# A four-layer conv/attention kernel: layer 0's products with v stored by channel instead of by row

## The chip, the cores and the metric

The kernel runs on one core of a Trainium2 chip. A core has five engines that work side by side, each with its own list of instructions: PE (TensorE, matmuls), DVE (VectorE, elementwise work and sums along a row), ACT (ScalarE, activations and copies), POOL (GpSimd, which here issues the indirect gathers) and SP (SyncE, which here issues plain DMAs). They wait for each other only through semaphores. On-chip memory (SBUF) has 128 partitions; an instruction of DVE works on all 128 at once and walks through the elements of each partition one after the other. PSUM is the small memory that PE writes into.

The metric is the device time of one execution in microseconds (us). Its median over 15 runs is 9,851.63 us before the change (9,807.8 to 9,883.81). A profile is taken in one more execution.

## What is computed

An input of 4 images, 64 x 64 pixels, 128 channels, float32, runs through four layers. The change is in layer 0, a deformable attention with 4 groups of 32 channels. For each pixel and group, 9 sampling points are displaced by learned offsets; each is interpolated from its 4 neighbouring pixels. The reference for it, cut to what matters:

```python
k_list, v_list = ([], [])
for i in range(G):                                  # G = 4 groups
    off = conv1x1(pconv(q_img, pconv_off_w[i]), w_off[i], b_off[i])
    dil = 2 * i + 1
    k_list.append(deform_sample(kv[0, :, i], off, mask, dil, dil * PAD))
    v_list.append(deform_sample(kv[1, :, i], off, mask, dil, dil * PAD))
...
attn = jax.nn.softmax(jnp.einsum('bgnc,bgckn->bgnk', qf, ks_), axis=-1)
out = jnp.einsum('bgnk,bgckn->bgnc', attn, vs_)
```

`deform_sample` gathers four corners for each of the K2 = 9 points and adds them up with bilinear weights. The kernel never forms the samples: for the scores it multiplies q with all 9 x 4 = 36 gathered rows of k, weighs the 36 sums and adds each four; for the output it multiplies the 36 gathered rows of v with 36 weights (softmax numerator times corner weight) and adds them up. Layers 1 to 3 (linear attentions, a mixture of experts, a spectral filter) follow, image by image.

## The kernel before

**Staging.** `hybrid` runs the images b = 0 to 3 one after the other through layer 0. For each there are 8 chunks (c) of 8 image rows, each with 4 tiles (t) of 128 pixels, each with 4 groups (g): 128 groups an image, 512 in all. `attend` handles one tile and yields after each group. At each yield `hybrid` inserts pieces of other work: the layers 1 to 3 of the image before (`Post.run(b - 1)`), or weight preparation while b is 0. After image 3's layer 0, layers 1 to 3 of image 3 run alone. `front(b + 1)` (group norm and convolutions of the next image, which fill the table that is gathered from) is inserted too.

**One group in `attend`.** POOL issues 9 indirect DMAs (L609), one for each sampling point; each fetches for 128 pixels 256 floats: 4 corners of 32 k values and 32 v values. They land in `gt`, a tile from a pool of three buffers, so the gathers run up to three groups ahead and then wait until DVE has read a buffer for the last time. DVE then does, in this order:

- `pr` (L618): k half of `gt` times q, 36 x 32 products
- `s4` (L623): sum over the 32 channels, 36 results, a reduction over elements that lie side by side
- L624, L626, L628: corner weights, sum over corners, and the maximum `mx`
- ACT makes `ex` = exp(sc - max) (L632)
- `aw` (L636): `ex` times corner weights, 36 weights, written into the PSUM tile `qa`
- `pv` (L641): v half of `gt` times `aw`, 36 x 32 products. This is the last reader of `gt`
- `o` (L644): sum over the 36 rows for each of 32 channels

A tile's last group is followed by the division by `den` (L649, L651). `pr` and `pv` live in a pool with one buffer each (`self.t1`). The tile framework sets the order in each engine's list; as built, DVE's list has the `pr` of the next group between `pv` and `o`, and the next group's `s4` right behind `o`. All arithmetic is float32.

**Order on ACT.** While the spectral filter of layer 3 runs beside layer 0, the class `Turns` keeps an order on ACT between the filter's copies (`y`, L1419, from PSUM to SBUF) and `ex`: each `ex` is issued after the last ACT instruction of the other work inserted before it, and each `y` after the last `ex`.

**Layout of the products.** `pv` is a tile of 36 rows of 32 channels: a row i of 32 floats, then the next. The product is written in that order, side by side. The sum walks it by channel: for each channel the 36 rows, 32 floats (128 bytes) apart.

**Other lines spoken of.** In `where`, the corner weights `cw` (L571) are written at every 4th float and `my` (L561) at every 2nd; `ix` (L549) reads two inputs at every 2nd float. L962 and L212 are memsets by DVE: of one float in each 129 (32 of them), and of two full rows of 66. L246 reads one input at every 9th float. L1405 and L1429 are PE's two kinds of matmul in the spectral filter.

Of the kernel before, what the change touches and what calls it, by code (L numbers as in the profile page):

```python
# [8 lines left out]
F32 = mybir.dt.float32  # L9
I32 = mybir.dt.int32  # L10
AF = mybir.ActivationFunctionType
ALU = mybir.AluOpType
AX = mybir.AxisListType
# [3 lines left out]
P = 128  # L17
# [13 lines left out]
K2 = 9  # L31
# [147 lines left out]
class Layer0:  # L179
# [416 lines left out]
    def attend(self, b, c, t):  # L596

        nc = self.nc
        blk = self.blk[b, c]
        o = blk.o  # L600

        qa = blk.qa[t // 2]
        q0 = t % 2 * C
        den = self.sm.tile([P, G], F32, tag="den", name="den")
        for g in range(G):
            gt = self.gp.tile([P, K2, 256], F32, tag="gt", name="gt")
            for i in range(K2):
                col = g * K2 + i
                nc.gpsimd.indirect_dma_start(  # L609
                    out=gt[:, i, :], out_offset=None, in_=self.tbl[b % 2][:, :],  # L610
                    in_offset=bass.IndirectOffsetOnAxis(
                        ap=blk.idx[:, t, col : col + 1], axis=0
                    ),
                )
            corners = gt.rearrange("p i (c s) -> p (i c) s", c=4)
            cw = blk.cw[:, t, g * K2 : (g + 1) * K2, :]
            pr = self.t1.tile([P, 4 * K2, 32], F32, tag="pr", name="pr")
            nc.vector.tensor_mul(  # L618
                pr, corners[:, :, 0:32],
                qa[:, q0 + 32 * g : q0 + 32 * g + 32].unsqueeze(1).to_broadcast([P, 4 * K2, 32]),  # L620
            )
            s4 = self.sm.tile([P, 4 * K2], F32, tag="s4", name="s4")
            nc.vector.tensor_reduce(s4, pr, AX.X, ALU.add)  # L623
            nc.vector.tensor_mul(s4, s4, cw.rearrange("p i c -> p (i c)"))  # L624
            sc = self.sm.tile([P, K2], F32, tag="sc", name="sc")
            nc.vector.tensor_reduce(sc, s4.rearrange("p (i c) -> p i c", c=4), AX.X, ALU.add)  # L626
            mx = self.sm.tile([P, 1], F32, tag="mx", name="mx")
            nc.vector.tensor_reduce(mx, sc, AX.X, ALU.max, negate=True)  # L628
            ex = self.sm.tile([P, K2], F32, tag="ex", name="ex")
            with self.turns.after("behind"):  # L630
                self.turns.mark()
                nc.scalar.activation(ex, sc, AF.Exp, bias=mx, accum_out=den[:, g : g + 1])  # L632
            self.turns.took("samples")
            a0 = 2 * C + g % 2 * 4 * K2
            aw = qa[:, a0 : a0 + 4 * K2]
            nc.vector.tensor_mul(  # L636
                aw.rearrange("p (i c) -> p i c", c=4), cw,
                ex.unsqueeze(2).to_broadcast([P, K2, 4]),
            )
            pv = self.t1.tile([P, 4 * K2, 32], F32, tag="pv", name="pv")  # L640
            nc.vector.tensor_mul(  # L641
                pv, corners[:, :, 32:64], aw.unsqueeze(2).to_broadcast([P, 4 * K2, 32]),
            )
            nc.vector.tensor_reduce(  # L644
                o[:, t, 32 * g : 32 * g + 32], pv.rearrange("p i s -> p s i"), AX.X, ALU.add
            )
            if g < G - 1:
                yield
        nc.vector.reciprocal(den, den)  # L649
        og = o[:, t, :].rearrange("p (g c) -> p g c", g=G)  # L650
        nc.vector.tensor_mul(og, og, den.unsqueeze(2).to_broadcast([P, G, 32]))  # L651
        yield
# [1186 lines left out]
```

## Time and profile before

| | us |
|---|---|
| median of 15 runs | 9,851.63 |
| lowest, highest | 9,807.8, 9,883.81 |
| the profiled execution | 9,820.63 |
| its span, first to last instruction | 9,818.9 |

The busy time of the engines in five stretches (the images of layer 0, and what lies around them), with the TensorE clock that the chip granted (1 is full speed):

| stretch, us | what runs | PE | DVE | ACT | POOL | PE clock |
|---|---|---|---|---|---|---|
| 0 to 278 | first front, tables | 216 | 49 | 100 | 29 | 0.98 |
| 278 to 1,935 | image 0 of layer 0, weights, front | 404 | 922 | 104 | 1,097 | 0.60 |
| 1,935 to 4,150 | image 1; layers 1 to 3 of image 0 | 1,463 | 1,090 | 578 | 1,103 | 0.79 |
| 4,150 to 6,358 | image 2; layers 1 to 3 of image 1 | 1,480 | 1,105 | 583 | 1,100 | 0.80 |
| 6,358 to 8,536 | image 3; layers 1 to 3 of image 2 | 1,292 | 1,089 | 550 | 1,076 | 0.74 |
| 8,536 to 9,819 | layers 1 to 3 of image 3 | 1,032 | 380 | 337 | 0 | 0.87 |

How to read what follows: a *group* of instructions is all that come from one line with one operation; its row gives the count, the busy time, the mean duration in ns, and the time that the engine stood idle right before them, with what ended it ("<-"). A row of the *waits* says who waited, for whom, how long in total, how many times, and the longest. "remote" means that the profile knows no instruction that released the wait. No engine is busy all the time; how long an instruction takes matters only where something waits for it.

### The profile page before, as it was taken

Reading aid. Unit: us, or ns where it says so; the run is one execution under the profiler, and the core shown is the slowest. Engines: PE = TensorE matmul, PEld = TensorE weight load, DVE = VectorE, ACT = ScalarE, POOL = GpSimd, SP = SyncE. Lnnn points to the kernel's source line nnn. Section 1 sums busy time; section 2 is a strip of 40 time slices with the busy share of each in tenths; the row PEclk is TensorE's granted clock in tenths of the full one; section 3 lists DMA queues with packets and bytes.
Section 4 is the critical chain, followed back from the end, with each engine's and each line's share of the span. In section 5 each row is a group of like instructions: output and inputs, shape, how many; then the busy total and the mean of one; then the engine's idle time right before and its main releaser. Section 6 shows DMA issues by size and latency. Waiting matters only on the chain.

```text
span 9818.9 us, 86706 instructions
## 1 busy us (share of the span) xinstructions
PE 5886.1 (60%) x30155; PEld 4073.1 (41%) x30155; DVE 4635.5 (47%) x7777; ACT 2252.1 (23%) x4160; POOL 4405.9 (45%) x4736
## 2 busy tenths in 40 slices
PE   7455100046675677746675767743455777657899
PEld 6242000035344555525344555522144555435676
DVE  1555555565464444466464444466354444343222
ACT  3100000023122222223122222213122222242222
POOL 0666666755534545555534554555435555300000
PEclk9677555567887888878787888865677888877999
DMA  6444333335645444445645444454635444434322
GB/s 214 141 126 118 104 102 101 102 99 149 204 129 144 117 117 119 112 134 157 190 139 146 114 122 114 114 134 133 193 110 149 118 111 115 133 106 126 107 69 80
DMA packets 1130830, 1255.00 MB, mean 128 GB/s; under 512 B 392478, under 2 KB 923161, under 8 KB 1126169
## 3 DMA queue, kind: packets, MB, share of 16 engines
q1 hardware_dynamic: 906797, 644.20, 24.0%
q0 software_dynamic: 221184, 604.27, 21.3%
q8 instruction: 239, 3.92, 0.2%
q14 instruction: 198, 1.62, 0.1%
q10 hardware_dynamic: 2412, 0.98, 0.0%
HBM read 1061.76 MB, written 187.22 MB: 127 GB/s over the span
## 4 chain that ended last, share of the span: by engine, by line
PE 23%; another core or an unknown queue 12%; ACT 5%; issue 5%; DVE 5%; DMA 3%; SPq 0%; POOL 0%; DVEq 0%; ACTq 0%
PE pa L1429 10%; PE pq L1405 4%; ACT y L1419 2%; DMA xin<-x 1%; PE ph L1114 1%; PE pm L427 1%; DVE o L644 1%; ACT ln L147 1%; PE pa L1225 0%; PE pn L1235 0%; PE pt L727 0%; PE pt L1123 0%; PE pq L862 0%; DVE pr L618 0%
## 5 line engine op out<-in xcount | busy, mean ns | idle before, releaser
L609 POOL DMA_INDIRECT gt<-tbl,idx x4608 | 4396.9, 954 | 4067.1 <-DVE pv L641 2280.2
L1429 PE MATMUL pa<-y,m 128*128 128x256 f32 x8192 | 2132.1, 411 | 239.2 <-issue 231.1
L1429 PEld LDWEIGHTS pa<-y,m 128*128 128x128 f32 x8192 | 1625.2, 204 | 725.0 <-issue 496.4
L1419 ACT COPY y<-pq 128x1024 f32<-128x1024 f32 x896 | 869.1, 1015 | 2365.0 <-remote 1401.0
L636 DVE TENSOR_TENSOR qa<-cw,ex 128x36 f32<-128x36 f32 x512 | 104.6, 204 | 2370.8 <-ACT ex L632 2223.6
L1405 PE MATMUL pq<-th,xh 32*128 32x256 f32 x8192 | 698.7, 442 | 642.1 <-ACT y L1419 402.3
L644 DVE TENSOR_REDUCE o<-pv 128x32 f32<-128x1152 f32 x512 | 1075.9, 2101 | 9.0 <-DVE qa L636 3.5
L618 DVE TENSOR_TENSOR pr<-gt,qa 128x1152 f32<-128x1152 f32 x512 | 690.5, 1349 | 224.2 <-DMA gt<-tbl,idx 208.1
L427 PE MATMUL pm<-wd,xT 128*128 128x256 f32 x2376 | 639.8, 420 | 252.7 <-ACT kv L438 142.4
L1405 PEld LDWEIGHTS pq<-th,xh 32*128 32x128 f32 x8192 | 422.5, 204 | 868.5 <-ACT y L1419 450.8
L641 DVE TENSOR_TENSOR pv<-gt,qa 128x1152 f32<-128x1152 f32 x512 | 691.9, 1351 | 40.1 <-DVE qa L636 12.8
L623 DVE TENSOR_REDUCE s<-pr 128x36 f32<-128x1152 f32 x512 | 688.3, 1344 | 1.8 <-DVE qm L874 0.9
L427 PEld LDWEIGHTS pm<-wd,xT 128*128 128x128 f32 x2376 | 487.4, 212 | 377.3 <-ACT kv L438 161.2
L632 ACT ACTIVATE ex<-sc,mx 128x9 f32<-128x9 f32 x512 | 156.9, 307 | 1170.3 <-DVE mx L628 519.4
L1416 DVE COPY y<-pq 128x1024 f32<-128x1024 f32 x128 | 156.7, 1225 | 466.1 <-ACT y L1419 466.1
L460 PE MATMUL pm<-xT,wd 128*128 128x512 f32 x576 | 296.1, 656 | 133.1 <-ACT qo L477 50.9
L578 PE MATMUL qa<-sident,qt 128*128 128x128 f32 x256 | 53.4, 334 | 423.8 <-issue 216.6
L1114 PE MATMUL ph<-w,pooled 128*1 128x512 f32 x512 | 244.0, 759 | 65.4 <-DMA w<-in_L_ffn_weight_dram 49.5
L502 PE MATMUL pm<-q,weff 128*81 128x512 f32 x192 | 137.7, 858 | 199.2 <-ACT xr L670 110.7
L660 PE MATMUL pt<-ident,o 128*128 128x128 f32 x128 | 36.1, 381 | 354.6 <-DVE o L651 144.3
L147 ACT ACTIVATE ln<-xin,ln,ln 128x128 f32<-128x128 f32 x512 | 211.6, 483 | 127.4 <-DMA xin<-x 99.4
L1128 DVE TENSOR_TENSOR g<-pt,b1T 128x16 f32<-128x16 f32 x64 | 11.2, 176 | 476.6 <-PE pt L1123 368.8
(373 smaller groups left out, 6322.0 us busy)
## 6 DMA issues: line engine op xcount, KB each, us to landing
w<-in_L_ffn_weight_dram SPq DMA_DIRECT2D x512, 256.0 KB
th<-th SPq DMA_DIRECT2D x512, 256.0 KB
gt<-tbl,idx POOLq DMA_INDIRECT x4608
xin<-x SPq DMA_DIRECT2D x256, 256.0 KB
x<-xin SPq DMA_DIRECT2D x160, 256.0 KB
tbl<-kv SPq DMA_DIRECT2D x264, 128.0 KB
th<-wx SPq DMA_DIRECT2D x32, 1024.0 KB
q<-qd SPq DMA_DIRECT2D x288, 64.0 KB
```

Of the source, the lines that this page charges most:

```text
L147: self.nc.scalar.activation(dst, src, AF.Identity, bias=self.shift[:, i : i + 1], scale=self.rstd[:, i : i + 1])
L427: nc.tensor.matmul(pm[:, t, :], lhsT=self.xf[:, at : at + P], rhs=self.wd[:, tap, C:], start=(t == 0 and tap == 0), stop=False,)
L460: nc.tensor.matmul(pv, lhsT=self.wd[:, tap, :C], rhs=self.xT[:, 8 * c + dy : 8 * c + dy + 8, dx : dx + HW], start=(tap == 0), stop=False,)
L609: nc.gpsimd.indirect_dma_start(out=gt[:, i, :], out_offset=None, in_=self.tbl[b % 2][:, :], in_offset=bass.IndirectOffsetOnAxis(ap=blk.idx ...
L618: nc.vector.tensor_mul(pr, corners[:, :, 0:32], qa[:, q0 + 32 * g : q0 + 32 * g + 32].unsqueeze(1).to_broadcast([P, 4 * K2, 32]),)
L623: nc.vector.tensor_reduce(s4, pr, AX.X, ALU.add)
L641: nc.vector.tensor_mul(pv, corners[:, :, 32:64], aw.unsqueeze(2).to_broadcast([P, 4 * K2, 32]),)
L644: nc.vector.tensor_reduce(o[:, t, 32 * g : 32 * g + 32], pv.rearrange("p i s -> p s i"), AX.X, ALU.add)
L1114: nc.tensor.matmul(ph[32 * j : 32 * j + 1, :], lhsT=pooled[:, 16 * j + q : 16 * j + q + 1], rhs=w1s[j], start=True, stop=True,)
L1405: nc.tensor.matmul(pq[:, r // 2, r % 2, :, pair, :], lhsT=xh[rows, 2 * (q % 4) + pair, :], rhs=t[rows, 2 * (q % 2) + pair, :].rearrange("p ...
L1419: nc.scalar.copy(to, src)
L1429: nc.tensor.matmul(pa[:, h * 2 * P : (h + 1) * 2 * P].rearrange("p (g x) -> p g x", g=8), lhsT=s.m[u][:, KC * kc + i, :], rhs=yv[:, i], st ...
```

## The change

`pv` becomes a tile of 32 rows (channels) of 36 elements. The product still goes through `gt` row by row, 36 rows of 32, but writes each element into its channel's row: one channel and the next lie 36 floats (144 bytes) apart. The sum then reads, for each channel, 36 elements that lie side by side. Inputs, sizes, results and the order of the additions stay the same.

```diff
-            pv = self.t1.tile([P, 4 * K2, 32], F32, tag="pv", name="pv")
+            pv = self.t1.tile([P, 32, 4 * K2], F32, tag="pv", name="pv")
             nc.vector.tensor_mul(
-                pv, corners[:, :, 32:64], aw.unsqueeze(2).to_broadcast([P, 4 * K2, 32]),
-            )
-            nc.vector.tensor_reduce(
-                o[:, t, 32 * g : 32 * g + 32], pv.rearrange("p i s -> p s i"), AX.X, ALU.add
-            )
+                pv.rearrange("p s i -> p i s"), corners[:, :, 32:64],
+                aw.unsqueeze(2).to_broadcast([P, 4 * K2, 32]),
+            )
+            nc.vector.tensor_reduce(o[:, t, 32 * g : 32 * g + 32], pv, AX.X, ALU.add)
```

## The prediction

> **What bounds the kernel now.** I read the costliest groups first, then the waits, then one stretch of the timeline, then the shapes that show what strides cost. Columns of a group: busy us, mean ns of one | idle us before it.
>
> ```profile
> L609 POOL DMA_INDIRECT gt<-tbl,idx x4608 | 4396.9, 954 | 4067.1 <-DVE pv L641 2280.2
> ...
> L644 DVE TENSOR_REDUCE o<-pv 128x32 f32<-128x1152 f32 x512 | 1075.9, 2101 | 9.0 <-DVE qa L636 3.5
> ...
> L641 DVE TENSOR_TENSOR pv<-gt,qa 128x1152 f32<-128x1152 f32 x512 | 691.9, 1351 | 40.1 <-DVE qa L636 12.8
> L623 DVE TENSOR_REDUCE s<-pr 128x36 f32<-128x1152 f32 x512 | 688.3, 1344 | 1.8 <-DVE qm L874 0.9
> ```
>
> The two sums read 1152 elements each. L623 reads them side by side: 1.344 us. L644 reads them 128 bytes apart (32 floats): 2.101 us. DVE is busy 47% of the span, so the 0.757 us between them is worth something only where DVE is what the others wait for. The waits (us in total, times, longest):
>
> ```profile
> POOL gt L609 <- DVE pv L641: 2280.2, 264, 111.4
> DVE qa L636 <- ACT ex L632: 2223.6, 268, 22.4
> ACT y L1419 <- remote: 1401.0, 153, 20.2
> ...
> ACT ex L632 <- DVE mx L628: 519.4, 66, 26.8
> ...
> ACT ex L632 <- DVE sc L626: 140.9, 21, 11.4
> ```
>
> It is a circle: the gathers on POOL wait for pv, which frees one of three gt buffers; pv's weights (qa) wait for ex on ACT; ACT's y stands ahead of ex in its queue and waits for something that has no name here. One turn of it in the timeline (start, us, what, idle before):
>
> ```profile
> 3312.65 1.35 DVE L641 TENSOR_TENSOR pv<-gt,qa 128x1152 f32<-128x1152 f32 x1
> ...
> 3314.28 0.95 POOL L609 DMA_INDIRECT gt<-tbl,idx  x1 [4.81 <-DVE pv L641]
> ...
> 3335.50 0.94 POOL L609 DMA_INDIRECT gt<-tbl,idx  x1 [0.30 <-issue]
> 3339.36 1.93 ACT L1419 COPY y<-pq 128x1024 f32<-128x1024 f32 x2 [19.70 <-remote]
> ...
> 3345.37 0.32 ACT L632 ACTIVATE ex<-sc,mx 128x9 f32<-128x9 f32 x1
> ...
> 3345.80 0.20 DVE L636 TENSOR_TENSOR qa<-cw,ex 128x36 f32<-128x36 f32 x1 [19.34 <-ACT ex L632]
> 3346.04 1.35 DVE L641 TENSOR_TENSOR pv<-gt,qa 128x1152 f32<-128x1152 f32 x1
> ...
> 3347.66 0.94 POOL L609 DMA_INDIRECT gt<-tbl,idx  x1 [11.22 <-DVE pv L641]
> ```
>
> pv ends at 3314.00, POOL starts 0.27 us later and issues 18 gathers, 1.25 us from start to start, to 3336.44. Only 2.9 us after its last one does y start, though the matmuls it reads had ended at 3320.1 by their rows. Then y, ex, qa, pv, and POOL starts again 33.4 us after the start before. In the stretch behind the last gather (8,536 us to the end) the list of ACT's waits has no "remote" entry at all; y waits there for PE by name. So I read: while gathers are under way a finished matmul often tells ACT so only when they have run dry. What the mechanism is, no row shows. But it puts pv on the path: a pv that ends d us later starts the gathers d later, and they end d later, and ex, and the next pv.
>
> The sum o (L644) isn't on that circle. DVE's order is pv, pr of the next group, o, s of the next group, three small ones, together 1.35+1.35+2.10+1.34+0.54 = 6.7 us, and the next group's nine gathers take 9 x 1.25 = 11.25 us. Where o's length does reach the path is where ex waits for DVE's mx or sc: 66 + 21 = 87 times.
>
> **The change part by part.** *Nothing moves.* Every engine's list of instructions is the same in number and order; only the 512 pv and 512 o change shape. No DMA, no wait is added or taken away, and pv takes as many bytes.
>
> *The sum o becomes a side-by-side read.* 1152 elements, as L623: 2.101 to 1.344 us, gain 0.757 each, 388 us of DVE work in 512. It reaches the path at the 87 waits above: 87 x 0.757 = 66 us. Bounds: 0 (hidden under the gathers everywhere) and 98 us (ex also waits 9 times for s of L623 and 34 times for nothing named, in the same list: 130 x 0.757). All 388 us can't be had while DVE idles half of the span.
>
> *The product pv writes across.* It reads as before, but each element now lands 144 bytes (36 floats) from the one before. The trace has no such write; the nearest rows:
>
> ```profile
> L571 DVE TENSOR_TENSOR cw<-up,my 128x144 f32<-128x144 f32 x64 | 23.3, 421 | 0.0
> ...
> L561 DVE TENSOR_TENSOR my<-up,mk 128x144 f32<-128x144 f32 x32 | 9.6, 302 | 0.0
> L549 DVE SCALAR_TENSOR_TENSOR ix<-fl 128x144 f32<-128x144 f32 x32 | 9.6, 301 | 0.0
> ...
> L962 DVE MEMSET ln<- 128x32 f32 x4 | 0.3, 85 | 0.0
> ...
> L212 DVE MEMSET xT<- 128x132 f32 x1 | 0.2, 168 | 0.0
> ```
>
> All have 144 elements but the memsets. L571 writes every 4th float (16 bytes apart): 421 to 426 ns. L561 writes every 2nd: 302. L549 reads two inputs at every 2nd and writes side by side: 301. So reads at every 2nd float are free, writes too, and the write at every 4th costs (423 - 302) / 144 = 0.84 ns an element. For 1152 elements that is 0.97 us: pv would take 2.32 us. From the other side, L962 writes 32 floats 516 bytes apart in 85 ns, just what a memset of 32 in a row would take (60 ns for two, 168 for 132: 0.83 ns each): there the wide write is free, and pv would stay at 1.35. Between them lies the price of the wide read, 0.657 ns an element or 0.757 us. I take 0.97, since L571 is the same operation on the same engine, with two inputs; a memset reads nothing. Upper end: twice that, 1.94 us, in case 144 bytes cost more than 16; nothing shows it, but L644's 128-byte read costs no more an element than the 36-byte read of L246 (371 ns for 128 against 286 for a side-by-side one: 0.66 ns), so distance beyond the first step hardly counts for reads.
>
> The Trainium skill has a rule that speaks against this change, in "Advanced Engine Details and Errata", section "Memory Cachelines": SBUF works in 16-byte lines, and an access that doesn't hit a line at least twice in a row pays. It makes no difference between reads and writes, so by it the write across pays as the read across did; it gives no figure. Priced like the read, the sum below would be 208 x 0.757 - 66 = +91 us rather than +136.
>
> *Where pv's price lands.* POOL waits for pv 264 times, 24 of them in batch 0 (up to 1,935 us, where POOL mostly issues without a break and is itself the bound at 11.25 us a group) and 240 in batches 1 to 3. Not all 264 turns are closed by a late "remote"; the 153 waits of y are those surely so, and in the others PE's own work may hide a later gather. I take the middle, 208 (bounds 153 and 264): 208 x 0.97 = +202 us. Behind pv in DVE's queue everything up to o comes 0.97 later, and behind o only 0.97 - 0.757 = 0.21 later; the 4.5 us by which 11.25 exceeds 6.7 cover that. Were that cover gone, it would be 0.21 us in each of 512 groups, 109 us.
>
> *The sum:* +202 - 66 = +136 us. The profiled execution took 9,820.6 us (span 9,818.9), so 9,957; it lies 31 us under the median of the 15 runs, 9,851.6. Against the median: **9,988, say 9,990 us**. Ends, if the write costs at least what the read did: 153 x 0.757 - 98 = +18 and 264 x 0.97 = +256, so 9,870 to 10,108.
>
> **The rivals.**
> *A, writes across are free* (as L962's). Then o's gain alone remains, on the 87 waits: 9,852 - 66 = 9,786, faster. The memset speaks for it, 128 cw instructions against. It decides the sign wherever the price of pv is under 66 / 208 = 0.32 us, a third of cw's price. Chance 0.20.
> *B, it comes out even:* the write costs about what the read did and PE, at a granted clock of 0.74 to 0.80 in batches 1 to 3, is what really closes most turns, so neither edit reaches the path: 9,852. For it: PE is busy 1,463 of 2,215 us in batch 1. Against: y waits for no named matmul 153 times. Chance 0.13.
> *C, the far write is dearer than the 16-byte one:* pv +1.94, 208 x 1.94 - 66 = +338, 10,190, and DVE's own chain reaches 7.9 us a group, still under 11.25. Against it: reads show no such growth. Chance 0.07.
> *That the change doesn't do what it says:* L623 shows the very read that o becomes, so I give it no share of its own.
>
> **How the numbers follow.** The forecast (slower, by pv's place on the circle) has 0.60, C 0.07, B 0.13, A 0.20. About 0.2% (20 us) is what a measurement of this kernel can tell from no change: faster 0.20, same 0.13, slower 0.67. Predicted time: the forecast's, 9,990. Range: from 9,800, which leaves out the larger half of A, to 10,090, which leaves out C and the last 18 us of the forecast's own range; the forecast's own range is 9,870 to 10,108.
>
> **What would show it.** pv (L641) at 2.1 to 2.4 us and o (L644) at 1.34; DVE's busy time up by about 109 us to 4,745; some 260 waits of POOL for pv, and its idle time up by over 100 us; a group of batches 1 to 3 from 17.2 us ((8,536 - 1,935) / 384) to about 17.5; the last 1,283 us, behind the last gather, as before. It is wrong if pv stays under 1.7 us (then A), or if pv is over 2.1 us and the time doesn't move (then the circle isn't closed by the gathers and B holds).

## The result and the profile after

| | before | after |
|---|---|---|
| median, us | 9,848.58 (31 runs) | 9,982.17 (6 runs) |
| lowest, highest | 9,807.8, 9,883.81 | 9,969.76, 9,995.17 |
| span of the profiled execution | 9,818.9 | 9,982.0 |

The ratio is 1.0137, with a 95% interval of 1.012 to 1.0154: the change makes the kernel 133.6 us slower. The forecast was 9,990 us, from 9,800 to 10,090.

The costliest groups of the kernel after, from its page (busy us, mean ns of one | idle us before it):

```profile
L609 POOL DMA_INDIRECT gt<-tbl,idx x4608 | 4406.5, 956 | 4221.5 <-DVE pv L641 2277.0
...
L641 DVE TENSOR_TENSOR pv<-gt,qa 128x1152 f32<-128x1152 f32 x512 | 1130.1, 2207 | 27.5 <-issue 9.6
...
L623 DVE TENSOR_REDUCE s<-pr 128x36 f32<-128x1152 f32 x512 | 688.4, 1344 | 4.1 <-issue 2.3
L645 DVE TENSOR_REDUCE o<-pv 128x32 f32<-128x1152 f32 x512 | 686.0, 1340 | 3.3 <-DVE qa L636 1.2
```

The sum o now costs what the other side-by-side sum (L623) costs, 0.761 us less than before; pv costs 0.856 us more. On DVE the two nearly cancel: 512 x 0.095 = 49 us. But POOL's idle time grew from 4,067.1 to 4,221.5 us. These 154 us are nearly all of the 163 us by which the span grew.

The waits of the kernel after (us in total, times, longest):

```profile
DVE qa L636 <- ACT ex L632: 2314.1, 293, 26.2
POOL gt L609 <- DVE pv L641: 2277.0, 237, 113.4
ACT y L1418 <- remote: 1481.3, 144, 21.2
...
ACT ex L632 <- DVE mx L628: 339.4, 64, 26.2
...
ACT ex L632 <- DVE s L623: 297.5, 22, 20.4
```

The same three stand on top, and the same circle joins them. One turn of it, from the timeline (start us, duration, engine, line, what; in brackets the idle time before it):

```profile
5410.63 2.22 DVE L641 TENSOR_TENSOR pv<-gt,qa 128x1152 f32<-128x1152 f32 x1
...
5413.12 0.95 POOL L609 DMA_INDIRECT gt<-tbl,idx  x1 [15.01 <-DVE pv L641]
...
5422.81 2.21 DVE L641 TENSOR_TENSOR pv<-gt,qa 128x1152 f32<-128x1152 f32 x1
...
5425.29 0.94 POOL L609 DMA_INDIRECT gt<-tbl,idx  x1 [1.14 <-issue]
...
5435.31 0.95 POOL L609 DMA_INDIRECT gt<-tbl,idx  x1 [0.31 <-issue]
5438.83 1.93 ACT L1418 COPY y<-pq 128x1024 f32<-128x1024 f32 x2 [16.29 <-remote]
...
5444.84 0.32 ACT L632 ACTIVATE ex<-sc,mx 128x9 f32<-128x9 f32 x1
...
5445.27 0.20 DVE L636 TENSOR_TENSOR qa<-cw,ex 128x36 f32<-128x36 f32 x1 [15.89 <-ACT ex L632]
...
5445.52 2.24 DVE L641 TENSOR_TENSOR pv<-gt,qa 128x1152 f32<-128x1152 f32 x1
...
5448.02 0.95 POOL L609 DMA_INDIRECT gt<-tbl,idx  x1 [11.77 <-DVE pv L641]
```

POOL starts 0.27 us behind the end of pv, issues 18 gathers until 5436.26, y starts 2.6 us later, then ex, qa, pv, and POOL starts again. Between the ninth and the tenth gather it stands still for 1.14 us instead of 0.30: a pv in the middle of the turn ends at 5425.02, and POOL goes on 0.27 us behind it. The turn takes 34.9 us, against 33.4 in the one shown of before. This is one example; the count over all of them stands below, among the reasons.

Behind the last gather nothing changed. The stretch from there to the end, in the windows (length, then busy us of PE, PEld, DVE, ACT and POOL with their instructions, granted clock, DMA share, GB/s):

```profile
8702.00:9982.00 1280.00, 1027.47 (x6403) 752.88 (x6403) 379.42 (x743) 338.02 (x555) 0.00 (x0) 0.87 0.37 104
```

It took 1,283 us before.

One thing has to be known for the experiments: the very same kernel before took 9,849 us in the runs of the result, about 7,787 us beside most experiments, and 9,962 us beside the last, the latter two on one and the same chip, so each kernel below is compared only with runs of the kernel before that were made beside it.

### The profile page after: what moved, and what is told of

Read it like the earlier page. It is cut to its first block, busy times and chain, and to the rows that moved or that the text cites. A ratio compares the mean times of both kernels' runs of the same rounds, so it can differ in the third digit from the quotient of the medians.

```text
span 9982.0 us, 86706 instructions
## 1 busy us (share of the span) xinstructions
PE 5905.3 (59%) x30155; PEld 4072.3 (41%) x30155; DVE 4652.0 (47%) x7777; ACT 2258.8 (23%) x4160; POOL 4415.5 (44%) x4736
## 4 chain that ended last, share of the span: by engine, by line
PE 34%; another core or an unknown queue 27%; issue 12%; DVE 9%; ACT 8%; POOL 4%; DMA 4%; SPq 1%; DVEq 0%; ACTq 0%; POOLq 0%
PE pa L1428 13%; PE pq L1404 6%; POOL gt L609 4%; ACT y L1418 4%; PE pm L427 3%; DVE pv L641 2%; PE pm L460 1%; DMA xin<-x 1%; DVE pr L618 1%; PE ph L1113 1%; DVE s L623 1%; DVE o L645 1%; DMA gt<-tbl,idx 1%; PE pt L726 1%
## 5 line engine op out<-in xcount | busy, mean ns | idle before, releaser
L609 POOL DMA_INDIRECT gt<-tbl,idx x4608 | 4406.5, 956 | 4221.5 <-DVE pv L641 2277.0
L641 DVE TENSOR_TENSOR pv<-gt,qa 128x1152 f32<-128x1152 f32 x512 | 1130.1, 2207 | 27.5 <-issue 9.6
L623 DVE TENSOR_REDUCE s<-pr 128x36 f32<-128x1152 f32 x512 | 688.4, 1344 | 4.1 <-issue 2.3
L645 DVE TENSOR_REDUCE o<-pv 128x32 f32<-128x1152 f32 x512 | 686.0, 1340 | 3.3 <-DVE qa L636 1.2
L460 PEld LDWEIGHTS pm<-xT,wd 128*128 128x128 f32 x576 | 113.5, 211 | 332.3 <-issue 193.0
```

Of the source, the lines that this page charges most:

```text
L460: nc.tensor.matmul(pv, lhsT=self.wd[:, tap, :C], rhs=self.xT[:, 8 * c + dy : 8 * c + dy + 8, dx : dx + HW], start=(tap == 0), stop=False,)
L609: nc.gpsimd.indirect_dma_start(out=gt[:, i, :], out_offset=None, in_=self.tbl[b % 2][:, :], in_offset=bass.IndirectOffsetOnAxis(ap=blk.idx ...
L641: nc.vector.tensor_mul(pv.rearrange("p s i -> p i s"), corners[:, :, 32:64], aw.unsqueeze(2).to_broadcast([P, 4 * K2, 32]),)
L645: nc.vector.tensor_reduce(o[:, t, 32 * g : 32 * g + 32], pv, AX.X, ALU.add)
```

## The experiments

### The kernels before and after once more

The first four experiments (told next) ran where the kernel before takes 7,787 us. So both kernels were profiled again under these conditions, the kernel after timed as well.

> The kernel before, for its trace under the conditions of this call: ratio 1. If it takes about 7,790 us, its rows should have no y that waits for nothing named, POOL should issue in long stretches, and a group of images 1 to 3 should take about 12.5 us instead of 17.2; if about 9,850 us, the same picture as in the profile before.

> The changed kernel itself, as a control: the four runs before this one took 7,787 us for the kernel before, not 9,849, and their traces have next to no copy that waits long behind a finished matmul. Theory (place): where ACT's copies again come late behind the gathers (kernel before at about 9,850 us), +133 us; where they don't (about 7,787 us), the circle isn't closed by the gathers, and the sum of the two halves measured there is left, +60 for both dear and -28 for both cheap, so about +32 us (ratio 1.004). Rival 'the price of the change is the same everywhere': +133 us in both cases.

Before: 7,789.96 us for this execution. After: 7,808.07 against 7,787.38 us, ratio 1.0027 (1.0017 to 1.0036), so +21 us instead of +134. The kernel before, first from its page (gathers; then the chain that ended last), then its waits:

```profile
PE 30%; POOL 30%; issue 14%; DMA 11%; DVE 10%; ACT 4%; SPq 1%; DVEq 0%; ACTq 0%; POOLq 0%
...
L609 POOL DMA_INDIRECT gt<-tbl,idx x4608 | 4401.0, 955 | 2038.9 <-issue 1344.1
```

```profile
ACT ex L632 <- DVE mx L628: 1825.4, 238, 19.6
POOL gt L609 <- issue: 1344.1, 4410, 0.9
ACT y L1419 <- PE pq L1405: 1171.7, 467, 16.1
...
POOL gt L609 <- DVE pv L641: 420.2, 43, 107.2
```

Here y never waits for something without a name: "remote" is gone from its rows, and 467 waits name the matmul. POOL is idle 2,039 us instead of 4,067, two thirds of that being the short pause between one gather and the next. The gathers themselves take as long (955 ns), and they now have 30% of the chain that ended last. POOL's idle time differs by 2,028 us between the two profiles of this program, and the spans differ by 2,031 (9,818.9 and 7,788.2). Under the first conditions there are 310 stops of POOL (gaps of over 0.6 us between one gather's end and the next one's start, counted in the trace), under the second 36.

The kernel after under the same conditions, from its page and its waits:

```profile
L609 POOL DMA_INDIRECT gt<-tbl,idx x4608 | 4397.9, 954 | 2048.7 <-issue 1335.6
```

```profile
POOL gt L609 <- DVE pv L641: 419.2, 48, 106.4
```

A tenth of the stops, a sixth of the price (about +32 us had been expected). This fits the reading that pv's length counts where POOL stops for it, though not in strict proportion, and the rival of one price everywhere is out.

### The two prices apart: one at a time

The lists of instructions of these four kernels (before, after and the two here) are the same in number and order, so they form a clean square. The first leaves pv writing across and makes the sum read across as well; the second leaves pv as before and makes the sum read side by side.

```diff
 # on the kernel after
+rows = pv.rearrange("p s i -> p (s i)").rearrange("p (i s) -> p s i", s=32)
-nc.vector.tensor_reduce(o[:, t, 32 * g : 32 * g + 32], pv, AX.X, ALU.add)
+nc.vector.tensor_reduce(o[:, t, 32 * g : 32 * g + 32], rows, AX.X, ALU.add)
 # on the kernel before
+side = pv.rearrange("p i s -> p (i s)").rearrange("p (s i) -> p s i", s=32)
-nc.vector.tensor_reduce(
-    o[:, t, 32 * g : 32 * g + 32], pv.rearrange("p i s -> p s i"), AX.X, ALU.add
-)
+nc.vector.tensor_reduce(o[:, t, 32 * g : 32 * g + 32], side, AX.X, ALU.add)
```

Both sums then add products that belong to different channels; their lengths, not their results, are what is asked.

> pv is written across as in the change, and o reads at a distance as before: the sum walks the same tile 128 bytes apart (so it adds other products than one channel's; the output is not the reference's). Theory (place: pv's price counts once for each turn of the circle gathers, late release of y, ex, pv; o's length counts only where ex waits for DVE): pv 2.21 us, o 2.10 us; the change plus what o's gain was worth, 133 + 66 = +199 us on 9,849, so about 10,050 (ratio 1.020). Rival 'DVE's total' (a microsecond on DVE counts alike wherever it stands): the change gave +133 us for a net 0.095 us a group, so 0.856 us a group would give +1,200 us. Rival 'o is hidden everywhere': the same as the change, 9,982.

> pv is written side by side as before, and o reads side by side: the sum adds for each result 36 neighbouring products instead of one channel's (the output is not the reference's). Theory (place): pv 1.35 us, o 1.34 us; only o's gain on the 87 waits of ex for DVE, -66 us, about 9,783 (ratio 0.993). Rival 'DVE's total': -1,000 us. Rival 'o is hidden everywhere': 9,849, no change.

Both dear: 7,847.29 against 7,786.82 us, ratio 1.0083 (1.0071 to 1.0096). Both cheap: 7,759.12, ratio 0.9966 (0.9955 to 0.9977). The two groups of the first, from its page:

```profile
L641 DVE TENSOR_TENSOR pv<-gt,qa 128x1152 f32<-128x1152 f32 x512 | 1131.2, 2209 | 10.9 <-DVE eq L876 0.8
L646 DVE TENSOR_REDUCE o<-pv 128x32 f32<-128x1152 f32 x512 | 1076.9, 2103 | 1.1
```

The medians, in us, each against the kernel before run beside it (the +21 is the kernel after of the section above, which ran on another chip than the two new ones):

| | o reads across (2.10 us) | o reads side by side (1.34 us) |
|---|---|---|
| pv writes side by side (1.35 us) | 0 | -28 |
| pv writes across (2.21 us) | +60 | +21 |

So pv's price is +60 or +49 us (down a column), o's gain is -28 or -39 us (along a row): both have the sign that the forecast gave them, and the price is the larger. The first kernel is dearer by 512 x 0.86 = 440 us of DVE's time and loses 60, so DVE's total is not what is paid for. The sizes that had been expected, +199 and -66 us, were missed; they had been worked out for the conditions of the result.

### The same price ahead of pv and behind it

An extra product of the length of pv's surcharge is put between qa and pv in one kernel, right behind pv in the other. It multiplies rows of pr, which nobody reads any more.

```diff
+nc.vector.tensor_mul(pr[:, :21], pr[:, :21], aw[:, :21].unsqueeze(2).to_broadcast([P, 21, 32]))
```

> The kernel before, with one more product on DVE (672 elements, side by side, about 0.85 us, result not used) between aw and pv, so that pv ends 0.85 us later; pv itself and o as before. Theory (place): what pv's price was worth in the change, +199 us, about 10,045 (1.020). Rival 'the write across disturbs others' (the landing gathers, or PE's reads): no write across here, so only the DVE chain to ex is longer, 87 x 0.85 = +74 us, about 9,923, or less. Rival 'DVE's total': about +1,200 us.

> The same extra product, but right behind pv (ahead of o; the next group's pr then stands behind o): DVE's time a group grows by the same 0.85 us and qa is held as long, but pv ends when it did. Theory (place): no turn of the circle grows, only the places where ex waits for DVE, 87 x 0.85 = +74 us, about 9,923 (1.0075), clearly under the pad before pv. Rivals 'DVE's total' and 'qa held longer': the same as the pad before pv, 10,045 or more.

Ahead: 7,809.24 against 7,786.82 us, ratio 1.0026 (1.0016 to 1.0035). Behind: 7,803.77, ratio 1.0017 (1.0007 to 1.0027). The intervals overlap, so the pair does not tell the places apart; +199 and +74 us had been expected. Nor is it a clean pair. The additional instruction moved others in the lists of DVE, ACT, PE and SP, and in the second kernel the sum o went ahead of the next group's pr. POOL's wait for pv shows it, in the waits of the first kernel and of the second:

```profile
POOL gt L609 <- DVE pv L644: 405.6, 101, 48.8
```

```profile
POOL gt L609 <- DVE pv L641: 439.1, 98, 50.6
```

About 100 waits, the longest 49 and 51 us, where the kernel before has 43 and 107. So this test of the place failed: it neither shows it nor refutes it. Why 0.85 us ahead of pv costs 22 us, where pv's own 0.86 costs 49 or 60, is not shown either. The question of place was taken up with the kernels that follow.

### More stops: two buffers instead of three

With two gt buffers POOL stops more often, whatever the conditions. If the price is paid once for each stop, it must grow with them; if it is a fixed sum, it must stay at 21 us.

```diff
-self.gp = ctx.enter_context(tc.tile_pool(name="l0g", bufs=3))
+self.gp = ctx.enter_context(tc.tile_pool(name="l0g", bufs=2))
```

> The kernel before with two gt buffers instead of three, so that POOL has to wait for pv more often. Theory (place): the price of pv is the number of POOL's stops times a part of its length; with three buffers and no late copies there are 37 stops (7,787 us), with two there should be 150 to 300, and the kernel 1 to 6% slower than before. It is the base for the next two.

> The changed kernel with two gt buffers; its lists of instructions are those of the kernel before with two buffers. Theory (place): the price of the change grows with the stops: by 0.4 to 0.6 us a stop (133 us for 300 stops where copies come late, 21 us for 37 where they don't) +60 to +180 us over two_bufs_before for 150 to 300 stops. Rival 'a fixed price, whatever POOL waits for' (the net 0.095 us a group, or a disturbance by the write across): +21 us again, at most +49.

With pv as before: 8,268.92 against 7,784.47 us, ratio 1.0625 (1.0609 to 1.0641), just above the 1 to 6% that had been expected. With pv writing across: 8,334.57, ratio 1.0708 (1.0692 to 1.0724). These two kernels have the same lists as each other. The gathers, from the page of the first and of the second:

```profile
L609 POOL DMA_INDIRECT gt<-tbl,idx x4608 | 4394.2, 954 | 2545.1 <-issue 1342.2
```

```profile
L609 POOL DMA_INDIRECT gt<-tbl,idx x4608 | 4389.1, 952 | 2594.7 <-issue 1324.9
```

The change now costs 66 us, with 153 stops of POOL in the trace of the first and 161 in that of the second. Set beside the other two pairs:

| conditions | POOL's stops, before and after | change costs, us | us for each stop of before |
|---|---|---|---|
| three buffers, 7,787 us | 36 and 37 | 21 | 0.58 |
| two buffers, 8,269 us | 153 and 161 | 66 | 0.43 |
| three buffers, 9,849 us | 310 and 299 | 134 | 0.43 |

A fixed sum is out. The cost goes with the stops, at about half a microsecond each. That is less than pv's 0.86; o's gain, -28 to -39 us in the square, is one reason, and how much of the difference it makes in each row was not measured.

### Release the buffer early

If it is pv's length as the last reader of gt that costs, gt can be released early instead. The first of the nine gathers that go into a buffer writes its first 4 rows only. Here pv is two products, the first over these 4 rows, the second over the other 32, and gt is one tile of three slots, so that each gather waits for those reads alone that its own rows have.

```diff
-gt = self.gp.tile([P, K2, 256], F32, tag="gt", name="gt")
+gt = self.gt[:, self.turn % 3]
+self.turn += 1
...
-nc.vector.tensor_mul(
-    pv, corners[:, :, 32:64], aw.unsqueeze(2).to_broadcast([P, 4 * K2, 32]),
-)
+for r0, r1 in ((0, 4), (4, 4 * K2)):
+    nc.vector.tensor_mul(
+        pv[:, r0:r1], corners[:, r0:r1, 32:64],
+        aw[:, r0:r1].unsqueeze(2).to_broadcast([P, r1 - r0, 32]),
+    )
```

> The kernel before, with the three gt buffers held in one tile and pv done in two pieces: 4 rows (128 elements, about 0.28 us), then 32 rows (1024 elements, about 1.22 us). The first of a group's nine gathers needs only the first piece done, the second the rest, so POOL can start again about 1.07 us sooner; DVE works 0.15 us longer a group. Theory (place), where copies come late behind the gathers: 208 to 233 turns of 1.07 us shorter, -222 to -249 us, and 87 x 0.15 = +13: about -220 us (ratio 0.978). Where they don't: POOL stops only some 100 times, so at most -100 us, and likely -20 to +10. Rival 'only the length of DVE's chain counts': +13 to +77 us, slower.

> The split pv (4 rows, then 32) with two gt buffers, so POOL is let go 1.07 us sooner at each stop. Theory (place): faster than two_bufs_before by 0.5 to 1 us a stop, 75 to 300 us, against 33 us with three buffers. Rival 'only DVE's chain counts': 0 to +77 us slower, since DVE works 0.15 us longer a group.

> The kernel before, with gt's three buffers as three slots of one tile, as in the split release, but with pv in one piece that reads all 36 rows. It asks what the gain of the split release (7,754.6 against 7,784.5 us, ratio 0.9958) came from. If the early release of gt made it, this kernel takes as long as the kernel before (ratio 1.000, within 0.001) and the list of POOL's waits for pv is the one of the kernel before. If the one tile or the other order of the lists made it, this kernel gains the same 0.4% without any split. A ratio between the two shares the gain out. Under the conditions of 9,849 us for the kernel before, the early release would be worth more, some 300 stops by 0.3 to 1.1 us, and this kernel would again stand at the kernel before.

Split with three slots: 7,754.57 against 7,787.38 us, ratio 0.9958 (0.9944 to 0.9971): -33 us, where -20 to +10 had been called likely. (The 7,784.5 us in the third expectation is the kernel before on a later occasion.) Split with two: 8,155.33, ratio 1.0484 (1.0468 to 1.05), 114 us under the two buffers without a split. The pieces of the first, by form:

```profile
L645 DVE TENSOR_TENSOR pv<-gt,qa 128x1024 f32<-128x1024 f32 x512 | 621.5, 1214 | 0.0
L645 DVE TENSOR_TENSOR pv<-gt,qa 128x128 f32<-128x128 f32 x512 | 145.7, 285 | 10.3 <-DVE eq L881 0.4
```

Their times add up to 1.50 us, 0.15 more than one pv, and the kernel is still faster. One restart in its timeline shows how POOL is let go earlier:

```profile
5272.08 0.20 DVE L639 TENSOR_TENSOR qa<-cw,ex 128x36 f32<-128x36 f32 x1
5272.32 1.42 DVE L645 TENSOR_TENSOR pv<-gt,qa 128x128 f32<-128x128 f32 x2
5272.88 0.94 POOL L612 DMA_INDIRECT gt<-tbl,idx  x1 [4.05 <-DVE pv L645]
5273.66 1.35 DVE L621 TENSOR_TENSOR pr<-gt,qa 128x1152 f32<-128x1152 f32 x1
5274.13 0.95 POOL L612 DMA_INDIRECT gt<-tbl,idx  x1 [0.30 <-issue]
```

The row of pv stands for both pieces, from 5272.32 to 5273.74. POOL starts 0.56 us behind their start, 0.27 us behind the end of the short one, while the long one still runs. The long one has ended when the second gather starts at 5274.13. Where the kernel before holds POOL up for 1.35 us and the kernel after for 2.21, this one does for 0.29. Over all stops the traces say the same: with two buffers, the piece of the stops that is pv goes from 207 us in all to 37 for the short product, and the stops together from 982 (153 of them) to 855 (145).

But the early release is not the only thing that differs. With pv in two pieces, the lists of DVE, ACT, PE and SP have another order than those of the kernel before. The control, one tile without a split, was to tell such things apart. It ran last, by chance under conditions in which the kernel before takes 9,962.22 us: it took 9,968.61, ratio 1.0004 (0.9986 to 1.0022). So the tile of slots is worth nothing that can be seen there. The order is another matter: in its trace the control has the lists of the kernel before, so the order that came with the split stays untested, as a rival for part of the 33 us and of the 114. The control was not run beside the split. Its waits:

```profile
POOL gt L612 <- DVE pv L644: 2444.1, 276, 112.2
DVE qa L639 <- ACT ex L635: 2328.3, 259, 24.1
ACT y L1422 <- remote: 1459.4, 149, 20.4
```

The circle is back, with 308 stops of POOL, on the chip that had shown 27 and 48 stops in the square's two kernels. The version with the split beats both kernels where it was run; it was not run with the circle closed.

### Length alone, by a read across

The product can also be turned around: it writes channel by channel, side by side, and reads the 36 elements of a channel 64 floats (256 bytes) apart. The products and their layout stay the same, the sum stays side by side, and so do the lists.

```diff
-    pv.rearrange("p s i -> p i s"), corners[:, :, 32:64],
-    aw.unsqueeze(2).to_broadcast([P, 4 * K2, 32]),
+    pv, corners[:, :, 32:64].rearrange("p i s -> p s i"),
+    aw.unsqueeze(1).to_broadcast([P, 32, 4 * K2]),
```

> The changed kernel, but pv walks channel by channel: it reads v across (256 bytes from element to element) and writes side by side, in the same layout and with the same result. pv should take 2.11 us (the across read's 0.657 ns an element) instead of 2.21, o 1.34. Theory (place): the price of pv, 49 to 60 us here for 0.856 us, becomes 43 to 53 us, less o's 28 to 39: +4 to +25 us on the kernel before, about +13 (ratio 1.0017). Rival 'the write across disturbs others, beyond its length': close to the kernel before or under it, -10 us or less.

7,799.76 against 7,784.47 us, ratio 1.0018 (1.001 to 1.0027): +15 us, and +13 expected. From its page:

```profile
L641 DVE TENSOR_TENSOR pv<-gt,qa 128x1152 f32<-128x1152 f32 x512 | 1087.6, 2124 | 11.0 <-DVE eq L875 0.8
...
L645 DVE TENSOR_REDUCE o<-pv 128x32 f32<-128x1152 f32 x512 | 688.6, 1345 | 1.0
```

pv's surcharge is 0.773 us here and 0.856 in the kernel after; the costs are 15 and 21 us, with overlapping intervals. As far as these intervals tell, and under these conditions, it doesn't matter whether pv is long by its write or by its read.

## Why the prediction was right

**The place of the cost: right, as the two recorded traces show.** Every stop of POOL in the two recorded traces can be cut into four pieces, from the end of the last gather to the start of the next:

| mean us of one stop | before (310 stops) | after (299 stops) |
|---|---|---|
| last gather's end to ex | 5.54 | 5.38 |
| start of ex to start of pv | 1.06 | 1.14 |
| pv | 1.35 | 2.21 |
| pv's end to the next gather | 0.29 | 0.31 |
| whole stop | 8.24 | 9.04 |

pv grew by 0.86 us; the other pieces moved by 0.16 at most, up or down. 299 stops, each 0.80 us longer, make +239 us; 11 stops fewer at 8.24 us make -91; together +149 (with rounding), of the 154 by which POOL's idle time grew. That the rest of the turn closes the circle, from a late matmul to POOL, is read from these traces and from its absence under the 7,787 us conditions: 186 of the 310 stops (1,836 of 2,555 us) hold a semaphore update that came over 2 us behind the modelled end of its matmul, 196 of the 299 after the change, and none of the 36 in the trace at 7,788 us. No experiment opened or closed the circle on purpose, and the one that moved the price ahead of pv and behind it did not tell the two apart.

**pv's price: mis-sized.** The step "L571 is the same operation on the same engine", 0.97 us, was 13% too high: 0.856 us, or 0.743 ns an element at 144 bytes, where L571 has 0.84 at 16. The price of the read across, 0.757, would have been too low. At 208 turns the term would have been 208 x 0.856 = +178 instead of +202. The Trainium skill ("Advanced Engine Details and Errata", section "Memory Cachelines") says that an access that doesn't hit a 16-byte line twice in a row pays, and it makes no difference between reads and writes. The runs agree that both pay here; they do not pay alike: 0.757 us for o's read at 128 bytes, 0.773 for v's at 256, 0.856 for the write at 144. The memset of the prediction, 85 ns for 32 floats 516 bytes apart, shows no such price.

**The turns: a middle that did not have to be the right one.** "208 (bounds 153 and 264)" counted waits. The traces have 310 and 299 stops, and some of them disappear as others grow longer. The lower bound took the 153 waits of y as turns that y surely closes; in the trace of before only 78 of these y start within a stop of POOL, the other 75 while gathers are still being issued, and in most stops with a late matmul it is another one than y's. The expected "some 260" waits of POOL for pv were 237, with 2,277 us behind them against 2,280, while POOL's whole idle time grew by 154 us, as said. So the number of waits that name pv is a poor count of the turns; the gaps between gathers are a better one.

**The gain of o: sign right, size not seen.** The term was -66 us. In the recorded pair, ex's waits for DVE's mx, sc and the two steps of s go from 106 (800 us) to 123 (905 us): no gain can be read there, and a later pv may make these waits longer as well. Alone it was only measured under the other conditions, at -28 and -39 us.

**The sum.** +136 forecast, +134 measured. With pv's true price the same working gives 178 - 66 = +112. So the closeness is partly luck: the price was 24 us too high, and 22 us the other way lie in the turns or in o's gain, which the recorded pair doesn't separate. By the stops the luck is larger: the longer stops cost 239 us, not 202, and 91 us came back through 11 stops that were no longer there, which the prediction has no term for; whether o's gain is behind these is not shown.

**What was to show it.** A group of images 1 to 3 took (8,702 - 1,945) / 384 = 17.6 us, where 17.5 was said. The last stretch stayed. DVE's busy time rose by 16.5 us on the page, not by 109: the groups' own rows add up to +438 and -390, so +48, and the page doesn't count twice what overlaps. The cover behind o, on which 109 us would have hung, held where it was tried, under the 7,787 us conditions: with o dear as well, DVE has 440 us more to do than before and the kernel loses 60.

**The rivals.** "Writes across are free" and "the far write is dearer" both fell with pv's row, 2,207 ns. "It comes out even" fell as stated: pv is over 2.1 us and the time moved. Nor is PE's granted clock needed as a reason: it fell from 0.766 to 0.758 in the recorded pair, but the kernel with both dear has 0.822 in its profile, against 0.823 in that of the kernel before at 7,788 us, and pays all the same.

**What stays open.** Why y's release comes late while gathers are under way, and why the same program on the same chip shows this at one time and not at another. The price of a pad ahead of pv against one behind it was not settled either, nor how much of the split's gain its other order makes.

## What to carry to other kernels

Here an elementwise product and a sum that traded a strided read for a strided write cost their engine about the same in all (0.095 us more in 3.5); what decided was which of the two releases a buffer that another engine stands still for. In such a case, keep the instruction that releases it short, put the stride in the one behind it, or let the last reader of the buffer be a small piece. Count the stops of the waiting engine, from the end of one of its instructions to the start of the next, and cut them into pieces: here that gave the price of the longer instruction better than the count of the waits that bear its name.

## What was not expected of the hardware

- The write across is cheaper an element at 144 bytes (0.743 ns over side by side, 2,207 against 1,351 ns for 1152) than at 16 bytes (0.83 to 0.86, 421 to 426 against 302 ns for 144), though it moves further.
- The same program differs by 28% in time, 7,787 to 9,962 us, on one chip. In the slower traces the semaphore of a matmul was updated over 2 us behind its modelled end 396 times (before, 3,215 us in all) and 446 times (after, 3,556 us), only 3 times in each once the last gather was issued; in the trace of before at 7,788 us it happened twice, and 400 times (3,195 us) in that of the control at 9,961 us. Of the 396, 275 came in a pause of POOL (over 0.4 us behind the end of a gather) and 121 while it was issuing, so many of these late updates, but not all, come when the gathers have run dry.
